# Start addresses of the weights, states and split activations in a recurrent layer with a quantized feed-forward

## The chip, the cores and the metric

The kernel runs on one core of a Trainium2 chip. Five engines work side by side and meet only through semaphores: TensorE (PE in the profile; its weight loads are listed apart as PEld), VectorE (DVE), ScalarE (ACT), GpSimd (POOL) and SyncE (SP), which here only issues DMAs. Operands lie in the on-chip buffer, 128 partitions wide; a tile takes the same byte range in each partition, so that a tile has one start address, counted in bytes within a partition. Matmul results go to a second buffer (PSUM). The metric is the device time of one execution in microseconds; three runs of the kernel before gave 541.5, 541.83 and 542.34, and the median is 541.83 us.

## The reference

The input `x` is 2 sequences of 1024 tokens of 512 values. First comes a recurrent layer, then a gated feed-forward with quantized weights; each is wrapped in layer norms and a residual:

```python
u = layernorm(x) @ W_in.T + b_in                     # 512 -> 1024
s_t = tanh(u_t + s_{t-1} * gamma + beta)             # along the 1024 tokens
x = x + layernorm(s @ W_out.T + b_out)               # 1024 -> 512
h = layernorm(x)
q = lambda w: w.astype(float8_e4m3fn).astype(float32)
gate = silu((h @ q(gate_w)) * gate_scale)            # 512 -> 1536
up = (h @ q(up_w)) * up_scale
x = x + layernorm(((gate * up) @ q(down_w)) * down_scale)   # 1536 -> 512
```

All of it is float32. The three quantized weights hold values that fit in 8 bits, kept as 4-byte numbers.

## The kernel before, in words

**Tiling.** The sequence is cut into 8 segments of 128 tokens that run side by side; 96 warm-up steps of the recurrence give each segment its starting state. Tokens are taken in 8 blocks of 256 rows (N = 256), each made of two tiles of 128 rows. P is 128, ND = 4 pieces of 128 of the model width, NH = 8 pieces of the hidden width, NI = 12 pieces of the feed-forward width.

**Early part** (the loop over `n` up to NB - 1). For each block, `norm`, `trans_x` and `copy_x` bring the normed input across (tile `xT`), `mm_u` (matmul at line 241) multiplies it with `win_sb` into `pu`, and `evac_u` writes the result to the states `us`. The recurrence runs at the same time on DVE and ACT (`warm_step`, then `main_step`). The weights of the feed-forward are loaded in pieces (`ws`), quantized on ACT (`q`) and expanded into `gate_sb`, `up_sb` and `down_sb`.

**Late part** (the loop over `i`, 96 + 2 iterations). One iteration is one of the 12 pieces `fc` of one of the 8 blocks `k`. PE's order in it is written out: `mm_g(i)` (line 452), then `down(i - 2, 0)` and `down(i - 2, 1)` (line 481), and at some `fc` the matmuls `mm_y` (line 403) or transposes of `h`. The activations are split into two parts of type `F32R`, a float32 form that PE takes in one pass, so that the sum of both is exact enough: `split_h` makes `hT` and `hL` of `h`, `f_in` and `f_low` make `fH` and `fL` of `f`. `mm_g` multiplies weights of gate, then of up, with `hT` and `hL` in turn: 2 x 4 x 2 = 16 matmuls of 256 columns, stationary a 128 x 128 piece of the weights (512 bytes in a partition), moving 256 columns of `hT` or `hL` (1024 bytes). `down` does 2 matmuls for each of the two tiles: stationary 128 columns of `fH` or `fL`, moving a row of `down_sb` with 512 columns (2048 bytes). So an iteration has 20 matmuls of F32R, each with a weight load of its own. `mm_u` and `mm_y` are plain float32 instead, and each matmul of the code stands as two in the profile.

**Addresses.** `tile_pool`s open one behind the other in a partition, and the tiles of a pool lie in the order in which the code first asks for each name, each rounded up to 32 bytes. Pools `const`, `weights`, `states` and `small` stay throughout; the pools of the early part are closed (`early.close()`), and `hw`, `xr`, `yw` and `fw` of the late part lie over them. In the program before, this gives the following starts, as the rest after division by 1024:

| tiles | start (bytes) | rest by 1024 |
|---|---|---|
| gate_sb, up_sb, down_sb (24,576 each) | 27104, 51680, 76256 | 480 |
| wout_sb | 100832 | 480 |
| us, 8 blocks of 8192 | 117216 and on | 480 |
| hT, two buffers; hL, two buffers (4096 each) | 187616 and on | 224 |
| xr (four buffers) | 204000 and on | 224 |
| fH, two buffers; fL, two buffers (1024 each) | 222432 and on | 224 |
| early part: win_sb, x, xT, ws | 187616 and on | 224 |

A piece of gate or up then starts 480 or 992 past a multiple of 1024, as `fc` is even or odd, since a row is 6144 bytes and a piece 512. Half a tile of `fH` or `fL` starts at 224 or 736.

Of the kernel before, what the change touches and what calls it, by code (L numbers as in the profile page):

```python
# [9 lines left out]
F32 = mybir.dt.float32  # L10
F32R = mybir.dt.float32r
# [7 lines left out]
P = 128  # L19
# [13 lines left out]
def segmented(  # L33
# [31 lines left out]
    N = K * GB  # L65
# [8 lines left out]
    def tokens(t, i):  # L74
# [6 lines left out]
    const = ctx.enter_context(tc.tile_pool(name="const", bufs=1))  # L81
    weights = ctx.enter_context(tc.tile_pool(name="weights", bufs=1))
    states = ctx.enter_context(tc.tile_pool(name="states", bufs=1))
    small = ctx.enter_context(tc.tile_pool(name="small", bufs=4))
# [17 lines left out]
    ffs = const.tile([P, 2, NI], F32, name="ffs")  # L102
    bout_bc = const.tile([P, D], F32, name="bout_bc")
    dsc_bc = const.tile([P, D], F32, name="dsc_bc")
    W_PIECE = 768
    pieces = [
        t.rearrange("p c n -> p (c n)")[:, i : i + W_PIECE]
        for t in (gate_sb, up_sb, down_sb)
        for i in range(0, ND * I, W_PIECE)
    ]  # L110
    n_sums = len(pieces)
    sums = const.tile([P, n_sums], F32, name="sums")

    def constants():
        make_identity(nc, ident)
        nc.gpsimd.memset(mhalf, -0.5)
# [50 lines left out]
    held = {}  # L167
# [221 lines left out]
    hw = late.enter_context(tc.tile_pool(name="hw", bufs=2))  # L389
    xr = late.enter_context(tc.tile_pool(name="xr", bufs=4))  # L390
    yw = late.enter_context(tc.tile_pool(name="yw", bufs=2))
    fw = late.enter_context(tc.tile_pool(name="fw", bufs=2))
# [71 lines left out]
    def f_in(i):  # L464
        f = held["f", i] = fw.tile([P, N], F32, tag="f", name=f"f_{i}")
        nc.vector.scalar_tensor_tensor(  # L466
            f, held["g", i][:, 1, :], ffs[:, 1, i % NI : i % NI + 1], held["gate", i], ALU.mult, ALU.mult
        )
        fH = held["fH", i] = fw.tile([P, N], F32R, tag="fH", name=f"fH_{i}")
        nc.scalar.copy(fH, f)  # L470

    def f_low(i):
        fL = held["fL", i] = fw.tile([P, N], F32R, tag="fL", name=f"fL_{i}")
        nc.vector.tensor_tensor(fL, held["f", i], held["fH", i].bitcast(F32), ALU.subtract)  # L474

    def down(i, j):
# [32 lines left out]
    def check_piece(n):  # L509

        junk = fw.tile([P, W_PIECE], F8, tag="junk", name=f"junk_{n}", bufs=1)
        nc.scalar.activation(
# [47 lines left out]
    for i in range(last + 3):  # L560
# [25 lines left out]
        if live:  # L586
            gate(i - 1)
            f_in(i - 1)
# [13 lines left out]
        if live:  # L602
            f_low(i - 1)
# [34 lines left out]
def rnn_then_quantized_glu(tc: tile.TileContext, *args):  # L638
    nc = tc.nc
    with tc.tile_pool(name="verdict", bufs=1) as pool:  # L640
        flag = pool.tile([1, 1], I32, name="flag")
        with tc.manual_schedule():
            redo, kept = segmented(tc, *args, flag, pool)
        with tc.If(redo > 0, preferred_fallthrough_block=True) as branch:
            sequential(tc, *args)
        with branch.Else():
            for dst, o in kept:
                nc.sync.dma_start(out=dst, in_=o)
# [367 lines left out]
```

## Time and profile before

The profiled execution took 541.67 us; the span from its first to its last instruction is 539.8 us.

| | PE | PEld | DVE | ACT | POOL |
|---|---|---|---|---|---|
| busy, us | 518.4 | 413.0 | 357.9 | 225.0 | 55.3 |
| share of the span | 96% | 77% | 66% | 42% | 10% |

The granted TensorE clock is 0.996 on average. Matmuls overlap in the profile: a duration of 0.28 us says how long one is on its way, while the next starts 0.12 us later. What a matmul costs a busy PE is therefore read from the distance between two starts in the timeline, not from the durations of a group; the ends are modelled.

### The profile page before, as it was taken

Reading aid. Unit: us, or ns where it says so; the run is one execution under the profiler, and the core shown is the slowest. Engines: PE = TensorE matmul, PEld = TensorE weight load, DVE = VectorE, ACT = ScalarE, POOL = GpSimd, SP = SyncE. Lnnn points to the kernel's source line nnn. Section 1 sums busy time; section 2 is a strip of 40 time slices with the busy share of each in tenths; the row PEclk is TensorE's granted clock in tenths of the full one; section 3 lists DMA queues with packets and bytes.
Section 4 is the critical chain, followed back from the end, with each engine's and each line's share of the span. In section 5 each row is a group of like instructions: output and inputs, shape, how many; then the busy total and the mean of one; then the engine's idle time right before and its main releaser. Section 6 shows DMA issues by size and latency. Waiting matters only on the chain. (4 is left out here: it accounts for less than half of the span.)

```text
span 539.8 us, 8063 instructions
## 1 busy us (share of the span) xinstructions
PE 518.4 (96%) x2818; PEld 413.0 (77%) x2818; DVE 357.9 (66%) x1014; ACT 225.0 (42%) x590; POOL 55.3 (10%) x152
## 2 busy tenths in 40 slices
PE   4999999999999899999999999999999999999992
PEld 3888877777447796699769778966987796689991
DVE  3588888886675768575856775585567556363734
ACT  1366666666324443344334333522533352123230
POOL 1200111100010101110110111010102101110101
PEclk9999999999999999999999999999999999999998
DMA  8563545322000000200200020020002001100101
GB/s 232 148 207 103 151 158 156 117 80 98 1 1 2 0 1 13 67 2 1 78 0 1 2 78 1 1 78 2 0 2 79 1 1 43 36 1 1 41 1 44
DMA packets 16113, 27.36 MB, mean 51 GB/s; under 512 B 1729, under 2 KB 4289, under 8 KB 16065
## 3 DMA queue, kind: packets, MB, share of 16 engines
q1 hardware_dynamic: 15632, 26.49, 17.1%
q8 instruction: 24, 0.39, 0.3%
q10 hardware_dynamic: 432, 0.27, 0.2%
q14 instruction: 25, 0.20, 0.1%
HBM read 22.57 MB, written 4.19 MB: 50 GB/s over the span
## 5 line engine op out<-in xcount | busy, mean ns | idle before, releaser
L241 PE MATMUL pu<-xT,win_sb 128*128 128x256 f32 x512 | 121.4, 388 | 1.3 <-ACT xT L233 0.5
L403 PE MATMUL py<-wout_sb,us 128*128 128x512 f32 x256 | 112.4, 593 | 1.0 <-DVE y L413 1.0
L241 PEld LDWEIGHTS pu<-xT,win_sb 128*128 128x128 f32 x512 | 94.9, 192 | 23.7 <-ACT us L250 11.3
L452 PE MATMUL pg<-hT,gate_sb 128*128 128x256 f32 x384 | 101.8, 298 | 0.0
L452 PE MATMUL pg<-hL,up_sb 128*128 128x256 f32 x384 | 96.3, 283 | 0.0
L452 PE MATMUL pg<-hT,up_sb 128*128 128x256 f32 x384 | 96.1, 283 | 0.0
L452 PE MATMUL pg<-hL,gate_sb 128*128 128x256 f32 x384 | 95.4, 281 | 0.0
L466 DVE SCALAR_TENSOR_TENSOR f<-pg,ffs,gate 128x256 f32<-128x256 f32 x96 | 46.1, 480 | 70.9 <-ACT gate L462 70.7
L403 PEld LDWEIGHTS py<-wout_sb,us 128*128 128x128 f32 x256 | 48.4, 190 | 56.4 <-issue 54.1
L283 ACT ACTIVATE us<-z 128x128 f32<-128x128 f32 x128 | 39.7, 310 | 100.1 <-DVE z L282 97.9
L481 PE MATMUL pd<-down_sb,fL 128*128 128x512 f32 x192 | 76.4, 398 | 1.6 <-DVE fL L474 1.6
L452 PEld LDWEIGHTS pg<-hL,gate_sb 128*128 128x128 f32 x384 | 72.4, 189 | 6.1 <-issue 2.9
L452 PEld LDWEIGHTS pg<-hT,gate_sb 128*128 128x128 f32 x384 | 72.3, 188 | 5.8 <-issue 3.1
L481 PE MATMUL pd<-down_sb,fH 128*128 128x512 f32 x192 | 75.4, 393 | 0.0
L452 PEld LDWEIGHTS pg<-hL,up_sb 128*128 128x128 f32 x384 | 73.5, 191 | 0.0
L452 PEld LDWEIGHTS pg<-hT,up_sb 128*128 128x128 f32 x384 | 73.4, 191 | 0.0
L462 ACT ACTIVATE gate<-pg,ffs 128x256 f32<-128x256 f32 x96 | 44.9, 467 | 67.0 <-PE pg L452 63.4
L470 ACT CAST fH<-f 128x256 fp32r<-128x256 f32 x96 | 39.0, 406 | 78.8 <-DVE f L466 77.5
L134 POOL TENSOR_SCALAR var<-mv 128x1 f32<-128x1 f32 x64 | 14.4, 224 | 471.7 <-DVE mv L132 470.8
L474 DVE TENSOR_TENSOR fL<-f,fH 128x256 fp32r<-128x256 f32 x96 | 40.2, 418 | 10.9 <-ACT fH L470 9.8
L280 DVE TENSOR_TENSOR z<-coef,us 128x128 f32<-128x128 f32 x127 | 36.3, 286 | 12.2 <-ACT us L283 12.0
L481 PEld LDWEIGHTS pd<-down_sb,fL 128*128 128x128 f32 x192 | 36.4, 190 | 7.4 <-DVE fL L474 2.8
(68 smaller groups left out, 498.6 us busy)
## 6 DMA issues: line engine op xcount, KB each, us to landing
xr<-in_x_dram SPq DMA_DIRECT2D x16, 256.0 KB, 3.9
out_dram<-o SPq DMA_DIRECT2D x16, 256.0 KB, 2.9
x<-in_x_dram SPq DMA_DIRECT2D x14, 256.0 KB, 8.9
ws<-in_gate_w_dram SPq DMA_DIRECT2D x12, 256.0 KB, 5.4
ws<-in_up_w_dram SPq DMA_DIRECT2D x12, 256.0 KB, 2.6
ws<-in_down_w_dram SPq DMA_DIRECT2D x12, 256.0 KB, 2.7
win_sb<-in_w_in_dram SPq DMA_DIRECT2D x4, 512.0 KB
wout_sb<-in_w_out_dram SPq DMA_DIRECT2D x4, 512.0 KB
```

The source lines that it names most:

```text
L134: nc.gpsimd.tensor_scalar(var, mv[:, 1:2], EPS, 1.0, ALU.add, ALU.mult)
L241: nc.tensor.matmul(pu[:, 0, :], lhsT=win_sb[:, dc, hc * P : (hc + 1) * P], rhs=held["xT", n][:, dc, :], start=(dc == 0), stop=(dc == ND - 1),)
L280: nc.vector.tensor_tensor(z, coef, run["state"], ALU.mult)
L283: nc.scalar.activation(u, z, AF.Tanh)
L403: nc.tensor.matmul(held["py", i], lhsT=of_tile(i, hc), rhs=wout_sb[:, hc, :], start=(hc == 0), stop=(hc == NH - 1),)
L452: nc.tensor.matmul(pg[:, n, :], lhsT=w[:, dc, fc * P : (fc + 1) * P], rhs=held[part, k][:, dc, :], start=(dc == 0 and part == "hT"), stop= ...
L462: nc.scalar.activation(g, held["g", i][:, 0, :], AF.Silu, scale=ffs[:, 0, i % NI : i % NI + 1])
L466: nc.vector.scalar_tensor_tensor(f, held["g", i][:, 1, :], ffs[:, 1, i % NI : i % NI + 1], held["gate", i], ALU.mult, ALU.mult)
L470: nc.scalar.copy(fH, f)
L474: nc.vector.tensor_tensor(fL, held["f", i], held["fH", i].bitcast(F32), ALU.subtract)
L481: nc.tensor.matmul(held["d", 2 * k + j], lhsT=held[part, i][:, j * P : (j + 1) * P], rhs=down_sb[:, fc, :], start=(fc == 0 and part == "fH ...
```

## The change

Two tiles that nothing reads or writes are asked for: `room1`, 136 float32 values (544 bytes) in the pool `const`, ahead of `sums`, and `room2`, 64 values (256 bytes) in the pool `small`, ahead of all others there. `fH` and `fL` are asked for from the pool `hw` instead of `fw`; both pools have two buffers for each name. No instruction is added, removed or moved.

```diff
     dsc_bc = const.tile([P, D], F32, name="dsc_bc")
+
+    const.tile([P, 136], F32, name="room1")
     W_PIECE = 768
...
     sums = const.tile([P, n_sums], F32, name="sums")
+
+    small.tile([P, 64], F32, tag="room2", name="room2", bufs=1)
...
-        fH = held["fH", i] = fw.tile([P, N], F32R, tag="fH", name=f"fH_{i}")
+        fH = held["fH", i] = hw.tile([P, N], F32R, tag="fH", name=f"fH_{i}")
         nc.scalar.copy(fH, f)
...
-        fL = held["fL", i] = fw.tile([P, N], F32R, tag="fL", name=f"fL_{i}")
+        fL = held["fL", i] = hw.tile([P, N], F32R, tag="fL", name=f"fL_{i}")
```

## The prediction

> **What bounds the kernel now.** I read first the busy rows and the slices, then busy times by stretch, then PE's timeline. In the page, PE's slices and the clock:
>
> ```profile
> PE   4999999999999899999999999999999999999992
> PEclk9999999999999999999999999999999999999998
> ```
>
> PE is full from the second slice to the last but one, at full clock. By stretches (columns: stretch, length, then busy us of PE, PEld, DVE, ACT, POOL):
>
> ```profile
> 164.00:200.00 36.00, 33.39 (x233) 30.00 (x232) 24.34 (x65) 16.71 (x43) 3.69 (x10) 1.00 0.00 1
> 200.00:528.00 328.00, 328.00 (x1935) 266.31 (x1934) 203.91 (x522) 120.70 (x308) 32.90 (x88) 1.00 0.08 22
> ```
>
> From 200 to 528 us PE is busy throughout, while DVE is busy 62%. The list of waits agrees: PE waits for others some 11 us in the whole run, 6.8 of them for the first input. The chain of waits itself holds only the last three DVE instructions, so it says nothing here. **The end is set by the distance between matmul starts.** PE's timeline (start, duration, line, operands), over the end of one iteration and the start of the next:
>
> ```profile
> 313.05 0.28 PE L452 MATMUL pg<-hL,up_sb 128*128 128x256 f32 x1
> 313.17 0.28 PE L452 MATMUL pg<-hT,up_sb 128*128 128x256 f32 x1
> 313.29 0.28 PE L452 MATMUL pg<-hL,up_sb 128*128 128x256 f32 x1
> 313.41 0.40 PE L481 MATMUL pd<-down_sb,fH 128*128 128x512 f32 x1
> 313.64 0.40 PE L481 MATMUL pd<-down_sb,fL 128*128 128x512 f32 x1
> 313.88 0.39 PE L481 MATMUL pd<-down_sb,fH 128*128 128x512 f32 x1
> 314.11 0.40 PE L481 MATMUL pd<-down_sb,fL 128*128 128x512 f32 x1
> 314.34 0.28 PE L452 MATMUL pg<-hT,gate_sb 128*128 128x256 f32 x1
> ```
>
> Starts are 0.12 us apart for 256 columns and 0.23 to 0.24 for 512. Taken over all such neighbours in the trace without a wait, the means are 119.1 ns (gate 118.4, up 119.8) and 232.5 ns. Plain float32 gives a row to hold this against, in merged runs:
>
> ```profile
> 46.24 1.89 PE L241 MATMUL pu<-xT,win_sb 128*128 128x256 f32 x8
> 304.63 6.60 PE L403 MATMUL py<-wout_sb,us 128*128 128x512 f32 x15
> ```
>
> Of the first run, 7 distances and the last duration (0.38) make 1.89: 216 ns. Of the second, 14 distances and a last 0.6: 429 ns. These go through their columns twice, so one pass costs 108.0 ns for 256 columns and 214.5 for 512. **The one-pass matmuls pay 11.1 and 18.0 ns more than this.** Each has its own weight load, which starts with the matmul ahead of it (load 313.41, `fL`; matmul 313.41, `fH`). That excess is all that start addresses could give back: 16 x 11.1 + 4 x 18.0 = 250 ns per iteration, 96 iterations, 24.0 us.
>
> **The change, part by part.** *Where tiles land.* `room1` adds 544 bytes ahead of the weights: gate_sb at 27648, up_sb 52224, down_sb 76800, us from 117760: all multiples of 1024. `room2` adds 256 more ahead of `hw`: 187616 + 800 = 188416 = 184 x 1024. In `hw`, 16,384 bytes of hT and hL are followed by fH at 204800 and fL at 206848, multiples again. But all that lay between fH and hT in the old order is a multiple of 1024 too, so the two pads alone would align fH and fL; the move to `hw` changes only higher bits of the address. Early tiles (win_sb, xT, x) are aligned as well. *Counts:* no instruction, semaphore owner or engine order changes; DMAs are the same in number and order. Two unused tiles cost no time.
>
> *Which tiles lie over which.* A late tile waits for the last reader of what lay there. `xr` 0 and 1 now lie over the third and fourth `x`, 2 and 3 over `xT`; their loads start at 125 us, the first use is at 148.7 us, and a load lands after 3.9 us, so a wait of up to 20 us would be covered. It would hold up later DMAs on SP's queue, and there is none urgent. fH and fL lie over the first two `x`, read long before. I take nothing; without that cover it would be the few us of the last `mm_u`.
>
> *DMA into aligned tiles.* [...] I take nothing, as it is nearest to what the other DMAs show: hidden under work.
>
> *DVE and ACT.* Their operands move too. PE does not wait for them after 200 us: between the end of fL and the matmul that takes it lie 2 us or more in nearly all iterations after the first block. A changed duration of some per cent there is hidden.
>
> *The matmuls.* No row of before has an aligned one-pass operand, so I bound this. Upper gain: the whole excess. But in the first block (164 to 200 us) PE is held by DVE: fL is often ready only 0.06 us ahead of its matmul. I credit 84 of 96 iterations: 84 x 250 = 21.0 us.
>
> [...]
>
> Which part of it hangs on the start? Split the excess into a part per 256 columns (a) and one per matmul (b): a + b = 11.1, 2a + b = 18.0, so a = 6.9 and b = 4.2 ns. What bytes cost as they pass stays wherever they start; what an operand costs once, for beginning off a boundary, would go. That is 20 x 4.2 = 84 ns an iteration, 84 iterations, **7.1 us**. Lower bound: b paid twice, 96 x 84 ns = 8.1 us lost, or more.
>
> **Sum.** 541.67 (profiled execution: span 539.8 and 1.9 around it) - 7.1 = 534.6. The median of the runs is 0.16 higher, so 534.7 is the forecast.
>
> **Rivals.** *The whole excess goes* (520.7 us). For: the plain passes, which have none, show that PE can read at this pace. Against: they take two passes for a load, so that a conflict may hide there, and their operands are no better aligned (rest 224 and 480).
>
> *Nothing moves* (541.7 us). For: in the up rows the distance stays at 120 ns in every iteration, although weights start at rest 480 or 992 by turns and the moving operand steps by 1024 from piece to piece. So the address bits of 512 and up have no effect on it, and only the rest by 512, one pair of values in the whole trace, could. Against: that pair is just what the change alters. That the unused tiles get no room and nothing moves would end here too.
>
> *Slower, by a meeting of the two reads* (549.8 us). Before, moving and stationary operand start 256 bytes apart by the rest of 512 (224 against 480 or 992; down the same with roles exchanged). After, they start 0 apart, and the load begins within 3 ns of the matmul ahead. If reads at the same rest get in each other's way, b is paid again, in all 96 iterations since a slower PE is late everywhere: 8.1 us. It decides as soon as the distance in the up rows goes above 120 ns. Against: the moving read runs ahead of the load and sweeps over all rests anyway; win_sb and xT are already 0 or 512 apart, and plain float32 shows no cost.
>
> **How the numbers follow.** The gain of part or most of b, up to some 13 us: 0.31. The whole or nearly: 0.17. Nothing: 0.22. Slower by a meeting or another effect of place: 0.30. Below 0.2% (1.1 us, about what a measurement of this kernel can tell from no change) counts as same: 0.48, 0.22, 0.30. The range has to hold cases of both signs: from 519.5, just under the whole excess, to 551, just over b paid twice; perhaps one chance in ten lies above it and one in thirty below. The likeliest case by itself is 528 to 540.
>
> **What would show it.** Right: instruction counts unchanged, gate and up distances near 115 ns, down near 228, plain matmuls still at 216 and 429. A distance of 109 means the whole excess went; 120 in the up rows that the start doesn't matter; above 120 a meeting. Wrong in another way: the stretch from 200 to 528 us no longer full on PE, or the time differing before 164 us, where no one-pass matmul runs.

## The result, and the profile after

The kernel after takes 541.97 us (median), the kernel before 542.02 in the same comparison: a ratio of 0.9998, with a 95% interval of 0.9988 to 1.0008. **The change moves every operand and changes nothing in the time.** The profiled execution of after has a span of 539.0 us.

The tiles do lie where the sum of sizes put them: gate_sb at 27648, hT from 188416, fH at 204800, all multiples of 1024. PE's timeline of after, over the end of one iteration and the start of the next (start, duration, line, operands):

```profile
312.26 0.28 PE L456 MATMUL pg<-hL,up_sb 128*128 128x256 f32 x1
312.38 0.28 PE L456 MATMUL pg<-hT,up_sb 128*128 128x256 f32 x1
312.50 0.28 PE L456 MATMUL pg<-hL,up_sb 128*128 128x256 f32 x1
312.62 0.40 PE L485 MATMUL pd<-down_sb,fH 128*128 128x512 f32 x1
312.85 0.40 PE L485 MATMUL pd<-down_sb,fL 128*128 128x512 f32 x1
313.08 0.39 PE L485 MATMUL pd<-down_sb,fH 128*128 128x512 f32 x1
313.31 0.40 PE L485 MATMUL pd<-down_sb,fL 128*128 128x512 f32 x1
313.55 0.28 PE L456 MATMUL pg<-hT,gate_sb 128*128 128x256 f32 x1
```

The steps, by which is meant the time from one matmul's start to the next, are the old ones, 0.12 us in the up rows and 0.23 to 0.24 in down. Over all steps of the trace that no wait breaks, the means are 119.1 ns for gate and up (119.1 before) and 232.5 for down (232.4 before), and 698 of the 768 up steps are exactly 120 ns (703 before). Of the two stretches that the prediction looked at, PE again fills the second and not the first (length, then busy us of PE, PEld, DVE, ACT, POOL):

```profile
164.00:200.00 36.00, 33.38 (x238) 30.39 (x237) 23.88 (x65) 17.15 (x44) 3.67 (x10) 1.00 0.00 1
200.00:528.00 328.00, 328.00 (x1933) 266.12 (x1931) 203.78 (x522) 120.55 (x308) 32.75 (x88) 1.00 0.08 22
```

In this profile the chain of waits is whole, and it names the bound that the prediction had to infer, PE with the matmuls of lines 456, 407 and 485 ahead (this is the page's share of the span by engine, then by line):

```profile
PE 69%; DVE 18%; ACT 7%; issue 3%; DMA 1%; POOL 1%; ACTq 0%; SPq 0%; DVEq 0%; POOLq 0%
PE pg L456 32%; PE py L407 17%; PE pd L485 16%; DVE zw L274 5%; ACT sw L276 5%; DVE zw L273 5%; PE pu L245 3%; DVE z L286 2%; DVE z L284 2%; ACT us L287 2%; PE ph L145 1%; DVE st L218 1%; DVE st L131 1%; DMA x<-in_x_dram 1%; DVE mv L136 1%
```

So two questions were left: do starts matter at all, and if so, why not here; and what are the 11 and 18 ns?

### The profile page after: what moved, and what is told of

The parts are those of the page before. It is cut to its first block, busy times and chain, and to the rows that moved or that the text cites. A ratio compares the mean times of both kernels' runs of the same rounds, so it can differ in the third digit from the quotient of the medians.

```text
span 539.0 us, 8061 instructions
## 1 busy us (share of the span) xinstructions
PE 517.9 (96%) x2818; PEld 412.8 (77%) x2818; DVE 357.7 (66%) x1014; ACT 224.9 (42%) x590; POOL 55.1 (10%) x152
## 4 chain that ended last, share of the span: by engine, by line
PE 69%; DVE 18%; ACT 7%; issue 3%; DMA 1%; POOL 1%; ACTq 0%; SPq 0%; DVEq 0%; POOLq 0%
PE pg L456 32%; PE py L407 17%; PE pd L485 16%; DVE zw L274 5%; ACT sw L276 5%; DVE zw L273 5%; PE pu L245 3%; DVE z L286 2%; DVE z L284 2%; ACT us L287 2%; PE ph L145 1%; DVE st L218 1%; DVE st L131 1%; DMA x<-in_x_dram 1%; DVE mv L136 1%
```

## Experiments

In what follows, *distance* is the start address of the moving operand less that of the stationary one in `mm_g`, by the rest of 256 (in `down` the roles are exchanged); *origin* is where the weights start. Before has distance 0 in this sense (224 against 480), and after too. The expectations, which are quoted as recorded, also call the step between two matmuls a distance.

### Do starts matter?

Two kernels came first. One puts the weights, hT and hL 4 bytes off, at mixed distances:

```diff
-    gate_sb = weights.tile([P, ND, I], F32R, name="gate_sb")
+    def off(t, n):
+        return t[:, 1 : 1 + t.shape[1] - 8].rearrange("p (c n) -> p c n", n=n)
+
+    gate_sb = off(weights.tile([P, ND * I + 8], F32R, name="gate_sb"), I)
...
-            held["hT", k] = hw.tile([P, ND, N], F32R, tag="hT", name=f"hT_{k}")
+            held["hT", k] = off(hw.tile([P, ND * N + 8], F32R, tag="hT", name=f"hT_{k}"), N)
```

(up_sb, down_sb and hL in the same manner.)

> The three quantized weights, hT and hL start 4 bytes past a multiple of 32, at other rests by 1024 than in both kernels; fH and fL at rest 448. Theory 1 (start addresses play no part at all): distances of matmul starts 120 ns in the up rows, mean of gate and up near 119, mean of down near 232.5, time within 0.2% of before. [...]

The other leaves the weights at a multiple of 1024 and puts h and f 160 bytes further:

```diff
-    small.tile([P, 64], F32, tag="room2", name="room2", bufs=1)
+    small.tile([P, 104], F32, tag="room2", name="room2", bufs=1)
```

> After, with 160 bytes more ahead of hw: weights at rest 0, hT, hL, fH and fL at rest 160, so that the two reads start 160 bytes apart instead of 0 or 256. Theory 1 (starts play no part): up rows at 120 ns, down mean 232.5, time within 0.2%. Theory 3 (the distance between the two reads matters, and 0 and 256 happen to cost the same): up rows move off 120 by 2 ns or more in either direction, 3 us or more in the time.

The first took 545.12 us, ratio 1.0061 (1.0044 to 1.0078), with gate and up at 120.5 and down at 236.2 ns. The second took 540.28 us, ratio 0.9973 (0.9963 to 0.9983), gate and up at 118.0, up no longer at a steady 120. Theory 1 falls: starts do matter, by some tenths of a per cent, and the change missed it. With 4 bytes off, 3.4 us were lost. Theory 3 held in kind but not in size: 1.5 us were won where 3 or more were expected to move.

### Which property of the starts

Three more values of `room2`, each in place of the 64 above: 72, 80 and 96 values give distances 32, 64 and 128.

> After, with room2 32 bytes larger: weights at rest 0, hT, hL, fH and fL at rest 32. Before, after and the run with rest 160 differ in how far apart the two reads of a matmul start: 256, 0 and 160. Theory D (what matters is the distance of the two starts by the rest of some period that divides 256, and the change left it at 0): a distance of 32 is a new one, so up rows leave the steady 120 ns; the mean of gate and up may be as in the run with 160 (118.2), or to either side, and the time moves by 1 to 4 us either way. Theory E (only the address bits of 128 matter): up rows at 120, time within 0.2% of before.

> After, with room2 64 bytes larger: distance of the two starts 64. Theory D with a period of 64: as after, up rows at a steady 120 ns, time within 0.2% of before. With a period of 128 or 256: up rows off 120. Theory E (only the bits of 128): 120.

> After, with room2 128 bytes larger: distance of the two starts 128. Theory D with a period of 64 or 128: as after, up rows at a steady 120 ns, time within 0.2% of before. With a period of 256, and by theory E: up rows off 120, gate and up mean about 118.2 as with 160, time about 0.3% below before.

And 88 values, distance 96; and `room1` at 144 values in place of 136, which moves weights, h and f together to rest 32, at distance 0:

> After, with room2 96 bytes larger: distance of the two starts 96, the last of the four multiples of 32 in a period of 128. Theory D: up rows off the steady 120 ns, gate and up mean between 116.5 and 118.5, time 0.2 to 0.5% below before. Theory F: h and f at rest 96 by 128, as in before, so 120 ns and the time of before.

> After, with room1 32 bytes larger, so that weights, hT, hL, fH and fL all start at rest 32: distance 0, but h and f at the place where the run with rest 32 was 0.5% faster. Theory D (the distance of the two starts counts, with a period of 128): up rows at a steady 120 ns, gate and up mean 119.1, time within 0.2% of before. Theory F (the place of h and f by itself counts, whatever the weights do): up mean about 116.7, time about 0.5% below before.

| kernel | origin by 256 | distance by 256 | mean step of gate and up, ns | of down, ns | us | ratio to before, 95% interval |
|---|---|---|---|---|---|---|
| before | 224 | 0 | 119.1 | 232.4 | 541.75 to 542.3 | 1 |
| after | 0 | 0 | 119.1 | 232.5 | 541.97 | 0.9998 (0.9988 to 1.0008) |
| both at 32 | 32 | 0 | 119.2 | 232.5 | 541.94 | 0.9996 (0.9985 to 1.0007) |
| 32 apart | 0 | 32 | 116.9 | 232.7 | 539.42 | 0.9953 (0.9937 to 0.9969) |
| 64 apart | 0 | 64 | 117.3 | 233.8 | 539.97 | 0.9965 (0.9955 to 0.9974) |
| 96 apart | 0 | 96 | 119.7 | 231.8 | 542.6 | 1.0009 (1.0000 to 1.0017) |
| 128 apart | 0 | 128 | 119.3 | 232.1 | 541.93 | 1.0001 (0.9992 to 1.0010) |
| 160 apart | 0 | 160 | 118.0 | 233.5 | 540.28 | 0.9973 (0.9963 to 0.9983) |

The runs were made in several comparisons, each with executions of before beside it, so the ratio is the figure to compare. The steps account for it: over the 84 iterations that PE bounds, 84 x (16 x the change of gate and up + 4 x the change of down) gives -2.9, -1.9, +0.6, +0.2 and -1.1 us for 32, 64, 96, 128 and 160 apart, and -2.6, -2.1, +0.3, -0.1 and -1.5 were measured (against medians of before of 542.02, 542.02, 542.3, 542.02 and 541.75).

Three rows at distance 0 and three different origins agree within 0.1 ns, and nearly in the number of up steps at exactly 120 ns (703, 698, 703). With h and f at rest 32 and the weights at rest 0, the kernel is 0.5% faster; move the weights to 32 as well and the gain is gone. That refutes theory F and confirms the heart of theory D: **among starts at multiples of 32, the distance of the two counts, not their place.** (Place was varied at distance 0 alone; all other distances have origin 0.) Neither expectation for 128 came true as a whole: the time is that of before, but only 211 of the 768 up steps are 120 ns, and the rest lie between 115 and 128. By its steps 128 is thus not the same case as 0, nor 160 (118.0 ns) the same as 32 (116.9), which speaks against a period of 128. A distance of 256 in before and of 0 in after have the same mean in gate and up, 119.1 ns, so 256 fits. Theory E falls with 32. For 96 a gain was expected, and there was none: the up steps left 120 ns, to both sides, and the mean rose by 0.6 ns. Why 32 is better than 96 no run here tells.

What a good distance looks like in PE's timeline (32 apart): the up rows step by 0.11 to 0.12 us, and the down row by 0.23.

```profile
311.96 0.28 PE L456 MATMUL pg<-hL,up_sb 128*128 128x256 f32 x1
312.08 0.28 PE L456 MATMUL pg<-hT,up_sb 128*128 128x256 f32 x1
312.20 0.28 PE L456 MATMUL pg<-hL,up_sb 128*128 128x256 f32 x1
312.31 0.39 PE L485 MATMUL pd<-down_sb,fH 128*128 128x512 f32 x1
312.54 0.39 PE L485 MATMUL pd<-down_sb,fL 128*128 128x512 f32 x1
```

The run with 4 bytes had mixed distances, so the offset was tried again with 256 bytes of padding a tile instead of 32 (64 values in place of 8), which leaves the distance in `mm_g` at 0:

> Before, with the three weights, hT and hL 4 bytes past their old rest by 128 (96 becomes 100), so that in mm_g the distance of the two starts stays 0 by 128; padding is 256 bytes a tile. In down the moving row is 4 bytes off the stationary fH and fL, which stay at rest 96. Theory D alone (only the distance counts): gate and up at 119.1 with up at 120, time within 0.2%. [...]

It took 548.13 us, ratio 1.0101 (1.0078 to 1.0123). In PE's timeline the up rows step by 0.12 to 0.13 us:

```profile
316.57 0.29 PE L455 MATMUL pg<-hL,up_sb 128*128 128x256 f32 x1
316.69 0.29 PE L455 MATMUL pg<-hT,up_sb 128*128 128x256 f32 x1
316.82 0.28 PE L455 MATMUL pg<-hL,up_sb 128*128 128x256 f32 x1
316.94 0.39 PE L484 MATMUL pd<-down_sb,fH 128*128 128x512 f32 x1
```

Gate and up are at 122.2 ns and down at 237.0, 3.1 and 4.6 ns over before. Over the 84 iterations this makes 84 x (16 x 3.1 + 4 x 4.6) = 5.7 us, and 5.8 were measured. Theory D alone falls: at the same distance, a start 4 bytes past a multiple of 32 is dearer. (In down the distance changes as well, by 4 bytes, so its 4.6 ns are not told apart.) Other offsets than 4 bytes were not run. Both kernels of this case start on multiples of 32, so the change had nothing to win there.

### What the 11 and 18 ns are

The load side, first. `mm_g` with half loads for hL, which leaves the low part of h out of half of the features:

```diff
-                for part in ("hT", "hL"):
+                for part in ("hL", "hT") if dc else ("hT", "hL"):
+                    c = P if part == "hT" else P // 2
                     nc.tensor.matmul(
-                        pg[:, n, :],
-                        lhsT=w[:, dc, fc * P : (fc + 1) * P],
+                        pg[0:c, n, :],
+                        lhsT=w[:, dc, fc * P : fc * P + c],
```

> Before, where the hL matmuls of mm_g load 64 weight columns instead of 128 and write 64 partitions, so that the low part of h is left out of half of the features; hL goes ahead of hT from the second piece on. Theory A (the excess over 108 ns is the price of the next weight load beside the stream): a matmul during which a 64-column load runs is followed after about 113 to 114 ns, half of the excess; one during which 128 columns are loaded after about 119. Theory B (the excess belongs to the one-pass stream itself): all stay at 118 to 120. Theory C (a weight load has a pace of its own, about 120 ns for 128 columns, and the matmul waits for it): 64-column loads give about 108, since the stream then is the longer one.

One execution took 537.5 us. The mean step of gate and up fell from 119.1 to 116.9 ns. With a quarter of the loaded columns gone, an excess in proportion to them would have fallen by a quarter of 11.1, to 116.3; so most of that drop is there. But it is not where theory A put it: a matmul beside a 64-column load is followed after 115 to 118 ns in the mean, one beside a full load after 117 to 118. The rows of down, whose own loads are unchanged, fell too, from 232.4 to 229.9. Theory B, that all stay at 118 to 120, and theory C, that the matmuls beside half loads take 108, fall as well. The price is not one of a single pair of load and stream; what carries it from one pair to others is not shown. The half loads also halve what those matmuls write, which this run cannot tell apart.

The stream side: the same matmuls in halves of 128 columns, each with a full load.

```diff
+            for c in (slice(0, P), slice(P, N)):
...
-                        pg[:, n, :],
+                        pg[:, n, c],
...
-                        rhs=held[part, k][:, dc, :],
+                        rhs=held[part, k][:, dc, c],
```

> Before, where mm_g streams 128 columns instead of 256 in each matmul, twice as many matmuls, each with a full load of 128 columns. Theory A (excess is the price of a load beside a stream): distance about 54 + 11 = 65 ns if the load could follow, more where it cannot. Theory B (excess belongs to the stream): half of 119, about 60, if the load could follow. Theory C (the load has a pace of about 120 ns): distance stays near 115 to 120 ns and the feed-forward takes about 1536 x 119 ns = 183 us more, the whole some 720 us.

One execution took 697.57 us, and the up rows step by 111.7 ns in the mean (110 the most frequent):

```profile
313.24 0.27 PE L453 MATMUL pg<-hL,up_sb 128*128 128x128 f32 x1
313.35 0.28 PE L453 MATMUL pg<-hT,up_sb 128*128 128x128 f32 x1
313.47 0.28 PE L453 MATMUL pg<-hL,up_sb 128*128 128x128 f32 x1
313.58 0.28 PE L453 MATMUL pg<-hT,up_sb 128*128 128x128 f32 x1
```

The stream alone would not need that long: 66 times, at the first matmul behind `down`, the step is 55 to 60 ns. So with a stream of half the length the load is the longer one and sets a pace of about 110 to 112 ns. Theory C is wrong in its figure: a load has a pace, but it is near the stream's 108 and not 120. With 128 and 256 columns the two are thus about equally long. That they hinder each other for this reason is not shown, and it cannot be all: `down` streams 512 columns, about twice as long as a load, and has the larger excess, while the plain rows of line 241, which also take 216 ns with one load of 4-byte weights each, have none.

Both at once: operands of 2 bytes, in the types and with the bitcasts of the old type gone.

```diff
-    gate_sb = weights.tile([P, ND, I], F32R, name="gate_sb")
-    up_sb = weights.tile([P, ND, I], F32R, name="up_sb")
-    down_sb = weights.tile([P, NI, D], F32R, name="down_sb")
+    gate_sb = weights.tile([P, ND, I], F16, name="gate_sb")
+    up_sb = weights.tile([P, ND, I], F16, name="up_sb")
+    down_sb = weights.tile([P, NI, D], F16, name="down_sb")
...
-        nc.vector.tensor_tensor(hL, held["ph", i], hT.bitcast(F32), ALU.subtract)
+        nc.vector.tensor_tensor(hL, held["ph", i], hT, ALU.subtract)
```

(hT, hL, fH and fL in the same manner.)

> Before, with gate_sb, up_sb, down_sb, hT, hL, fH and fL of type float16 instead of F32R: operands of 2 bytes, so that both reads of a matmul are half as long; the split into two parts keeps some 22 bits. Theory A (the excess over 108 and 214.5 ns is the price of two 4-byte reads side by side): distances fall to about 109 and 216 ns, 1536 x 10 + 384 x 17 = 22 us of PE time, some 19 us less in the time: about 522 us. Theory B (the excess belongs to one pass with a load of its own, whatever the type): distances stay near 119 and 232 and the time within 3 us of before.

**522.62 us, ratio 0.9655 (0.9632 to 0.9678).** In PE's timeline of this kernel the up rows step by 0.11 us, and down by 0.21 to 0.22:

```profile
321.16 0.27 PE L453 MATMUL pg<-hL,up_sb 128*128 128x256 f16 x1
321.27 0.27 PE L453 MATMUL pg<-hT,up_sb 128*128 128x256 f16 x1
321.38 0.27 PE L453 MATMUL pg<-hL,up_sb 128*128 128x256 f16 x1
321.49 0.38 PE L482 MATMUL pd<-down_sb,fH 128*128 128x512 f16 x1
321.71 0.38 PE L482 MATMUL pd<-down_sb,fL 128*128 128x512 f16 x1
321.92 0.38 PE L482 MATMUL pd<-down_sb,fH 128*128 128x512 f16 x1
322.14 0.38 PE L482 MATMUL pd<-down_sb,fL 128*128 128x512 f16 x1
```

The means are 109.2 and 216.0 ns, close to the 108.0 and 214.5 that half a plain row takes: the excess is gone. That a plain row goes through its columns twice was the author's reading; the runs show that it takes 216 and 429 ns where a 2-byte row of as many columns takes 109.2 and 216.0. The weight loads are shorter too, 98 ns each where before has 188 to 191. These are groups of loads, with busy us and mean ns behind the bar, two of before and then two of this kernel:

```profile
L452 PEld LDWEIGHTS pg<-hL,up_sb 128*128 128x128 f32 x384 | 73.5, 191 | 0.0
L452 PEld LDWEIGHTS pg<-hT,gate_sb 128*128 128x128 f32 x384 | 72.3, 188 | 5.8 <-issue 3.1
```

```profile
L453 PEld LDWEIGHTS <-up_sb 128*128 128x128 f16 x768 | 75.1, 98 | 8.7
L453 PEld LDWEIGHTS <-gate_sb 128*128 128x128 f16 x768 | 75.1, 98 | 29.8 <-issue 7.4
```

PE time saved is 1536 x 9.9 + 384 x 16.4 = 21.5 us, of which 84/96 are 18.8; 19.4 were measured. Theory B falls, and theory A's 522 us were met. The run changes load and stream together, and with the number of bytes also the type, so it does not say which of these would have been enough. That the excess comes from two 4-byte reads side by side is thus not proved, and the plain rows, which also have both and pay nothing, would need a reason of their own. It is also the version that beats both kernels, at another precision of the split, and with the range of half floats. A last run asks whether distance matters there too (32 bytes more in `small`, as `room2` of 8 values):

> The float16 kernel with 32 bytes more ahead of hw, so that the two reads start 32 apart by the rest of 128 instead of 0. If the loss is all from two 4-byte reads side by side, there is none left to save: distances 109.2 and 216 ns, time within 0.3% of the float16 run (522.6 us). If the distance also matters at 2 bytes: faster by 0.3% or more.

It took 523.39 us, ratio 0.9653 (0.9636 to 0.9670), at 109.2 and 216.0 ns: at 2 bytes this distance does nothing.

## Why the prediction was wrong

- **What bounds the kernel** was right. PE is busy 328.00 of 328.00 us between 200 and 528, and every kernel with other addresses moved as its steps did.
- **Addresses, overlaps, unused tiles, DVE and ACT** were right: no wait took the place of another, and the stretches before 200 us kept their busy times within 0.7 us. The aligned DMAs were priced at nothing; PE's first transpose came at 6.29 us in after against 6.76, but the run with both at 32 has 6.84, and other kernels 6.6 to 7.3, so no effect of alignment is shown.
- **The excess** was right in size: 21.0 us was the sum with the first block left out, and half floats, which took nearly all of it away, gave back 19.4. The credit of 84 of 96 iterations fits within a few per cent. As a ceiling for what start addresses give it was far too high: the best placement found gave 2.6 us.
- **The step that failed** is an assumption of the author's, which the runs do not bear out: "What bytes cost as they pass stays wherever they start; what an operand costs once, for beginning off a boundary, would go." It took the rest by 1024 for the boundary and priced b, 4.2 ns a matmul, as what would go: steps near 115 and 228 ns and a gain of 7.1 us. Measured were 119.1 and 232.5 ns, and no gain. Origins 224, 32 and 0 give the same steps, so there is no cost here for starting off a multiple of 1024. A start 4 bytes past a multiple of 32 does cost 3.1 ns, but no operand of before starts so. What else hangs on addresses is the distance of the two starts, which the change left at 0 by 256. Nor is b a cost paid once by each matmul that a better start takes off: such a cost would move gate, up and down by the same amount, but at 64 apart gate and up fall by 1.8 ns while down rises by 1.4. The 7.1 us were what a split of two rows into two unknowns left over, and no run changed that part alone.
- **The rival that nothing moves** came true, and its ground was half right: address bits of 512 and up have no effect in the up rows (703 of the 768 steps are 120 ns; the other 65, which it passed over, are 117 or 118). The answer to it, that the pair of 224 and 480 "is just what the change alters", was the misreading. By the rest of 256, 224 and 480 are the same value: the change turned a distance of 256 into one of 0, and these are one case. The prediction compared both numbers by the rest of 512 alone; before has no other distance, so its trace could not have told it better. That the result is nothing is in part a chance of the sizes chosen: with 32 bytes more in `room2` the kernel is 0.5% faster.
- **The rival of the two reads meeting** named the right quantity, the distance of the two starts, but on a ground that is wrong (0 is no worse than 256), and with a price of 8.1 us. The largest effect of distance found among starts at multiples of 32 is a gain of 0.47%, some 2.6 us.
- **Where the excess comes from** the runs narrow and do not settle: half a load on every other matmul takes 2.2 ns off the mean step, and the distance of the two starts moves it by as much. With operands of 2 bytes the excess is gone, at 109.2 ns for 256 columns and 216.0 for 512.

## What to carry to other kernels

Before pricing an alignment, ask which quantity the trace can tell of: write down the starts of both operands that are read side by side (in before, a load and the matmul ahead of it both start at 313.41 us), and test whether the change alters their distance by some small period, rather than their rest by a round number. In this kernel operands of 2 bytes were worth 3.5%, where their precision and range suffice, and the best placement of 4-byte operands 0.5%. A cost found by splitting two rows into two unknowns is not a cause until a run changes one of the terms alone.

## What the runs showed of the hardware

- One-pass 4-byte matmuls of 256 columns with a load each step by 116.9 to 119.7 ns in the mean on starts at multiples of 32, by 232 to 234 for 512 columns, and by 112 for 128 columns in the up rows; at 2 bytes the steps are 109.2 for 256 and 216.0 for 512. The plain float32 rows beside them stay at 216 and 429 in before and after, and at 429 with half floats and with 4 bytes off at an unchanged distance (eight in 3.60 us, of which the last has 0.6).
- In the up rows at distance 0 the steps settle at 120 ns at the three origins tried; at 32, 64, 96, 128 and 160 they do not.
- With both operands 4 bytes past a multiple of 32, at an unchanged distance, a matmul of 256 columns takes 3.1 ns more.
